# Seven block products for eight in the last 1x1 convolution of four images

## The chip, the cores and the metric

The kernel runs on one core of a Trainium2 chip, in fp32. A core has TensorE (matrix products into PSUM, an accumulator memory of 8 banks of 128 x 512 fp32), VectorE, ScalarE and GpSimd (the row POOL), and SyncE (SP); each takes its instructions in order from its own queue. Data moves between the chip's memory (DRAM) and the on-chip SBUF by DMA transfers that SP, ScalarE or POOL issue. The metric is the time of one execution on the device in microseconds (us), median of several runs.

## What is computed

Two bottleneck layers follow one another on 16 images of 1024 channels and 32 x 32 pixels. The first has a local self-attention in its middle, the second a 3x3 convolution:

```python
def layer0(x):                                  # self-attention bottleneck
    h = relu(bn(conv1x1(x, w_conv1)))           # 1024 -> 256
    h = self_att(h, wq, wk, wv, ...)            # 3x3 neighbourhoods, softmax over 9 taps
    return relu(bn(conv1x1(h, w_conv3)) + x)    # 256 -> 1024

def layer1(x):                                  # convolution bottleneck
    out = relu(bn(conv1x1(x, w1)))              # 1024 -> 256
    out = relu(bn(conv3x3(out, w2)))            # 256 -> 256
    out = bn(conv1x1(out, w3))                  # 256 -> 1024
    return relu(out + x)                        # x is layer0's output
```

The change is in the last convolution of `layer1` (w3), its addition of the residual x and its relu. Per image that is a 1024 x 256 matrix (the norm's scale is multiplied into it beforehand) times 256 x 1024 pixels.

## The kernel before

**Tiling.** Channels lie on the 128 partitions. A chunk is 128 channels of 1024 channels, so an image's input, output or residual is 8 chunks of 128 x 1024. A 256-channel tensor is a tile of 128 x 2 x 1024. A product is 128 x 128 weights times 128 x 512 pixels (half an image).

**Stages and order.** Nothing is ordered by a compiler's scheduler: the kernel issues every instruction in the order of a written list, `stages` (L974): `P` an image's first convolution and projections, `F` the fused end of layer 0 with the beginning of layer 1 (`fused`, L1065), `W` the 3x3 convolution of four images at once in Winograd's form (`winograd_conv`, L747), `U` the last convolution of one image (`last_sum`, L1106). The list's last line is

```python
"F12 F13 F14 U10:0123 F15 U10:4567 U11:01234 W12 U11:567 U12 U13 U14 U15",
```

so after `W12` (images 12 to 15) come chunks 5 to 7 of image 11 and then four whole `U` stages. VectorE's long work (the softmax, the attention sums, the Winograd transforms) is put between these stages by a small planner, the class `Side`, that keeps two clocks of estimated time (`side.passes`, with an estimated 3.43 us per chunk, `CHUNK`). By `U12` it has nothing left to place.

**A chunk of the last convolution** (class `Expand`, L371). `seed` (L379) lets ScalarE copy the residual chunk from SBUF into a PSUM tile of 128 x 1024 (two banks; the pool `psum` has four such tiles, all of PSUM); `products` (L386) adds four products to it; `result` (L401) lets ScalarE add the norm's shift, clip at zero and write a tile of SBUF (`rpool`, four tiles), in another order of the pixels, and POOL issues the store. `last_sum` calls `seed` two chunks ahead; `seeds` (L1119) names the first two of the next stage, so that a stage's end preloads for the next. The very last chunk is split: ScalarE takes half (L412) and VectorE half (L413), with a store from ScalarE's and one from SP's queue (L414, L415).

**Residuals.** Layer 0's output goes to DRAM and comes back. `loads` is one list in order of use, of the inputs, the Winograd forms (`V`) and the residuals (`r`). `more_loads` (L314) issues the next loads on POOL's queue as long as a room is free; the rooms are the five tiles of `xpool` (`CHUNKS`), counted by `live`. `seed` frees a room as soon as its residual is copied.

**Weights.** `more_weights` loads weight tiles through SP's queue; the two halves of the last convolution's weights (`u3`) are in SBUF from `U10:0123` on and are kept to the end.

**Between.** `finish_winograd` (L860) lets ScalarE apply norm and relu to an image's hidden tile after the 3x3 convolution, two instructions of 128 x 1024 in place (L863). `run` (L1129) calls it one part before a `U` stage ends, for the image of the next one.

Of the kernel before, what the change touches and what calls it, by code (L numbers as in the profile page):

```python
# [72 lines left out]
def sa_bottleneck_kernel(ctx: ExitStack, tc: tile.TileContext, x, w1t, wqkvt, w3t, u1t, u2t, u3t, params, out):  # L73
# [11 lines left out]
    zpool = ctx.enter_context(tc.tile_pool(name="zpool", bufs=3))  # L85
    psum = ctx.enter_context(tc.tile_pool(name="psum", bufs=4, space=bass.MemoryType.PSUM))
    dram = ctx.enter_context(tc.tile_pool(name="dram", bufs=1, space=bass.MemoryType.DRAM))


# [224 lines left out]
    def more_loads():  # L314

        while loads and live[0] < CHUNKS + RESULTS - 1:
            kind, b, c = loads[0]

            spare = kind == "x" and b < 2 and c >= CHUNKS
            if live[0] >= CHUNKS and not (kind == "x" and b < 2):  # L320
                return
# [11 lines left out]
            name = f"{kind}_{b}_{c}".translate(str.maketrans(" ,", "__", "()"))  # L333
            if spare:
                t = rpool.tile([P, HW], F32, tag="r", name=name)
            else:
                t = xpool.tile([P, NK * 2 * PART], F32, tag="x", name=name)
                t = t if kind == "V" else t[:, :HW]

            (nc.scalar if kind == "x" and b == 0 else nc.gpsimd).dma_start(t, src)  # L340
            loaded[loads.pop(0)] = t
            live[0] += 1

    def free():
# [774 lines left out]
    def seeds(at):  # L1119

        if at < len(stages):
            kind, b, of = stages[at]
            if kind in ("fused", "u3"):
                return [(expand("w3" if kind == "fused" else "u3", b), o) for o in of[:2]]
        return []

    hooks = {}

    def run(at):  # L1129
# [8 lines left out]
        if kind == "fused":  # L1138
            parts, count = fused(b, of, then), 2 * NC
        elif kind == "u3":  # L1140
            parts, count = last_sum(b, of, then), len(of)
        elif kind == "conv1":
            parts, count = first_conv(b), NC
        elif kind == "qk":
            parts, count = projections.setdefault(b, project(b)), 5
        elif kind == "v":
            parts, count = projections[b], 2
        else:
            side.finish_firsts()
            parts, count = winograd_conv(b), 18  # L1150
        alone = kind not in ("fused", "u3")
        for part in range(count):
            if alone and then and part >= count - 2 and kind != "wino":
                into, which = then[part - count + 2]

                if which not in into.ahead:
                    into.seed(which)
            if made and (kind, part) in (("conv1", 4), ("u3", count - 2)):
                finish_winograd(made.pop(0))
            cost = next(parts)  # L1160
# [75 lines left out]
```

## Time and profile before

| | |
|---|---|
| median of 3 runs | 2411.03 us (2407.73 to 2412.01) |
| profiled execution | 2409.75 us |
| its span | 2408.0 us |
| TensorE (PE) busy | 2380.5 us, 99% of the span |
| VectorE (DVE) busy | 2080.2 us, 86% |
| ScalarE (ACT) busy | 919.2 us, 38% |
| POOL busy | 466.0 us, 19% |
| `U12` to `U15` on TensorE | 2293.3 to 2403.2 us |
| a residual's load, from issue to landing | median 5.6 us |

The span is the time between the first and the last instruction of the profiled execution. In rows of instructions, `out<-in` are tiles, then comes the shape, then the count; at the end stands the idle time before it and what released it. PEld is the loading of weights into TensorE, which overlaps the products. An fp32 product is two passes, so it stands twice in the counts. In the slices each digit is the busy share of a fortieth of the span in tenths.

### The profile page before, as it was taken

The numbers are of one execution on the slowest core, as the hardware profiler recorded it, in microseconds if no ns is written. First come the engines' busy times: TensorE is split into PE (matmuls) and PEld (weight loads), VectorE is DVE, ScalarE is ACT, GpSimd is POOL, SyncE is SP. The second block draws the span as 40 slices with busy tenths as digits, with TensorE's granted clock in tenths as the row PEclk, the third lists the DMA queues.
The fourth block names the chain that finished last, engine by engine and source line by source line (L and its number), as shares of the span: only waits on it lengthen the run. The fifth ranks groups of instructions, "written<-read, shape, count | busy, mean of one in ns | idle before, by whom it ended". The sixth has DMA issues, their size and how long they took to land.

```text
span 2408.0 us, 18460 instructions
## 1 busy us (share of the span) xinstructions
PE 2380.5 (99%) x6144; PEld 1152.8 (48%) x6144; DVE 2080.2 (86%) x1648; ACT 919.2 (38%) x889; POOL 466.0 (19%) x854
## 2 busy tenths in 40 slices
PE   8999999999999999999999999999999999999999
PEld 3444444444476444444476444444476444434844
DVE  4799999999999999998999999999989999873700
ACT  3323241333122574442122574334122553344265
POOL 2111111111111232111111231111111221112132
PEclk9999999999999999999999999999999999999999
DMA  9979686888798897777898997787798986788887
GB/s 352 356 225 312 244 284 216 264 296 261 276 327 272 321 398 292 234 262 238 244 316 295 300 406 276 249 285 263 241 324 297 322 329 228 243 286 271 320 298 252
DMA packets 296126, 691.04 MB, mean 287 GB/s; under 512 B 20064, under 2 KB 166496, under 8 KB 287584
## 3 DMA queue, kind: packets, MB, share of 16 engines
q0 software_dynamic: 119024, 471.40, 54.4%
q1 hardware_dynamic: 175568, 213.97, 28.2%
q10 hardware_dynamic: 1440, 4.51, 0.5%
q8 instruction: 49, 0.80, 0.1%
q14 instruction: 45, 0.37, 0.0%
HBM read 416.09 MB, written 273.70 MB: 286 GB/s over the span
## 4 chain that ended last, share of the span: by engine, by line
PE 85%; DVE 5%; DMA 4%; issue 4%; POOL 1%; ACT 1%; SPq 0%; POOLq 0%; ACTq 0%; DVEq 0%
PE ps L358 35%; PE ps L390 29%; PE ps L454 11%; PE ps L771 9%; DVE acc L631 2%; DVE acc L649 1%; PE ps L492 1%; DMA a<-a 1%; DMA U<-uw 1%; POOL out_dram L418 1%; DMA a<-acc 1%; POOL r L340 1%; DMA uw<-u 0%; DMA s<-in_x_dram 0%; DMA v<-v 0%
## 5 line engine op out<-in xcount | busy, mean ns | idle before, releaser
L390 PE MATMUL ps<-a,w 128*128 128x512 f32 x1024 | 461.6, 596 | 5.8 <-ACT a L675 5.8
L358 PE MATMUL ps<-result,u 128*128 128x512 f32 x1024 | 459.9, 595 | 4.0 <-ACT result L417 4.0
L358 PE MATMUL ps<-x,w 128*128 128x512 f32 x1024 | 444.5, 595 | 6.4 <-DMA x<-in_x_dram 6.4
L390 PE MATMUL ps<-y,u 128*128 128x512 f32 x1024 | 441.2, 593 | 1.0 <-ACT ps L381 1.0
L631 DVE TENSOR_TENSOR acc<-e,bnv 128x2048 f32<-128x2048 f32 x144 | 327.6, 2283 | 34.1 <-ACT e L613 31.0
L574 DVE TENSOR_TENSOR prod<-qc,bnk 128x2048 f32<-128x2048 f32 x144 | 324.1, 2288 | 1.7
L417 ACT ACTIVATE result<-ps,par 128x1024 f32<-128x1024 f32 x128 | 142.4, 1113 | 462.2 <-PE ps L390 393.6
L390 PEld LDWEIGHTS ps<-a,w 128*128 128x128 f32 x1024 | 195.7, 191 | 253.9 <-issue 243.2
L358 PEld LDWEIGHTS ps<-x,w 128*128 128x128 f32 x1024 | 195.7, 191 | 251.9 <-issue 251.6
L358 PEld LDWEIGHTS ps<-result,u 128*128 128x128 f32 x1024 | 195.1, 191 | 250.5 <-issue 237.5
L390 PEld LDWEIGHTS ps<-y,u 128*128 128x128 f32 x1024 | 194.8, 190 | 245.6 <-issue 240.8
L649 DVE TENSOR_TENSOR acc<-acc 128x2048 f32<-128x2048 f32 x128 | 293.4, 2292 | 4.4
L454 PE MATMUL ps<-h,wqk 128*128 128x512 f32 x512 | 222.3, 592 | 0.0
L417 ACT ACTIVATE result<-ps,bn_sh 128x1024 f32<-128x1024 f32 x127 | 141.0, 1111 | 140.1 <-PE ps L390 139.6
L418 POOL DMA_DIRECT2D r<-result x128 | 68.8, 537 | 636.0 <-ACT result L417 620.5
L579 DVE TENSOR_TENSOR prod<-prod 128x2048 f32<-128x2048 f32 (+1 forms) x80 | 166.2, 2078 | 2.5
L454 PEld LDWEIGHTS ps<-h,wqk 128*128 128x128 f32 x512 | 97.3, 190 | 122.4 <-issue 109.9
L1037 ACT ACTIVATE h<-ps,par 128x1024 f32<-128x1024 f32 x32 | 38.5, 1203 | 279.1 <-PE ps L358 279.0
L381 ACT ACTIVATE ps<-r 128x1024 f32<-128x1024 f32 x128 | 130.5, 1020 | 27.1 <-DMA r<-r 19.6
L466 ACT ACTIVATE kp<-ps,par 128x1024 f32<-128x1024 f32 x64 | 77.4, 1209 | 156.4 <-PE ps L454 114.7
L381 ACT ACTIVATE ps<-s 128x1024 f32<-128x1024 f32 x128 | 131.1, 1025 | 2.5
L340 POOL DMA_DIRECT2D x<-in_x_dram x120 | 63.7, 531 | 301.0 <-PE ps L358 227.1
(317 smaller groups left out, 2296.6 us busy)
## 6 DMA issues: line engine op xcount, KB each, us to landing
s<-in_x_dram POOLq DMA_DIRECT2D x128, 512.0 KB, 6.3
r<-result POOLq DMA_DIRECT2D x128, 512.0 KB, 4.0
r<-r POOLq DMA_DIRECT2D x128, 512.0 KB, 6.5
out_dram<-result POOLq DMA_DIRECT2D x127, 512.0 KB, 6.2
x<-in_x_dram POOLq DMA_DIRECT2D x120, 512.0 KB, 5.1
v<-v SPq DMA_DIRECT2D x96, 408.0 KB, 4.6
U<-uw SPq DMA_DIRECT2D x72, 512.0 KB, 4.3
bnk<-kp SPq DMA_DIRECT2D x32, 680.0 KB, 7.7
```

Source lines behind the costliest of these rows:

```text
L340: (nc.scalar if kind == "x" and b == 0 else nc.gpsimd).dma_start(t, src)
L358: nc.tensor.matmul(ps[n][:, halves(half)], wt[:, c % (NC // 2), n * P : (n + 1) * P], src[:, halves(half)], start=(c == first), stop=(c == ...
L381: nc.scalar.activation(ps, loaded.pop((self.kind, self.b, o)), AF.Identity)
L390: nc.tensor.matmul(self.ahead[o][:, halves(half)], pieces[key][:, n, o % (NC // 2) * P :][:, :P], self.src[:, n, halves(half)], start=Fals ...
L417: nc.scalar.activation(to_, ps, RELU, bias=self.shift(o), scale=1.0)
L418: nc.gpsimd.dma_start(to, t)
L454: nc.tensor.matmul(ps[:, halves(half)], pieces[key][:, m, at : at + P], h[:, m, halves(half)], start=(m == 0), stop=(m == NW - 1),)
L574: nc.vector.tensor_tensor(by_row(t[:, two]), by_row(qc), kc[:, :, i : i + JROWS, j : j + W], ALU.mult)
L579: nc.vector.tensor_add(u[:, :, 0:4], u[:, :, 0:4], u[:, :, 4:8])
L631: nc.vector.tensor_tensor(by_row(dst), rows(e[:, k, :]).unsqueeze(1).to_broadcast([P, HEAD_DIM, JROWS, W]), vc[:, :, i : i + JROWS, j : j ...
L649: nc.vector.tensor_add(acc, acc, t)
L771: nc.tensor.matmul(acc[i][:, at, :, n, :], pieces[key][:, m, at, n * P : (n + 1) * P], v[:, at, :, m * (TILES + TR) :][:, :, :TILES], star ...
```

## The change

For images 12 to 15 two chunks of the output (256 channels, one *pair*) are computed together. Seen as blocks, a pair's weights are 2 x 2 blocks of 128 x 128 and the hidden tile is 2 x 2 blocks of 128 x 512 (two channel halves, two pixel halves). Four output blocks take eight products; the changed kernel uses Winograd's form of Strassen's scheme: seven products of sums of blocks.

- `late_weights`: at the start of `W12` VectorE makes the four sums of weight blocks (`s`) for all pairs, eight instructions. It also hands out SBUF that the attention no longer uses: four areas for sums of hidden blocks, five further rooms for residuals (`late_rooms`).
- `change`: VectorE makes an image's four sums of hidden blocks (t1 to t4, t4 in place of a block), for image 12 ahead of `U12`, for the others during the image before.
- `Pair`: products 1, 6 and 5 add up in one bank, 7 and 4 in another, 2 and 3 have one each; two such sets of four banks take the place of the pool `psum`, which is closed before `U12`. VectorE adds banks 1, 6, 5 (twice), 7, 4 and 2 into the residual tiles in SBUF. Product 3 is added to a half residual that ScalarE copied into its bank, and ScalarE copies the sum back. `result` then reads the residual tile. Product 5 of a pair and its results come after product 1 of the next pair. The last pair of all has an order of its own, and its product 2 adds to a half copied into the bank.
- `late_sums` takes the place of `last_sum` and of the preloads (`seeds`) for these images, and calls `finish_winograd` for the next image at an image's first pair.
- `free_late`: a residual's room comes free when its result is issued.

```diff
--- before.py
+++ after.py
@@ -83,8 +83,9 @@
     apool = ctx.enter_context(tc.tile_pool(name="apool", bufs=1))
     ppool = ctx.enter_context(tc.tile_pool(name="ppool", bufs=2))
     zpool = ctx.enter_context(tc.tile_pool(name="zpool", bufs=3))
-    psum = ctx.enter_context(tc.tile_pool(name="psum", bufs=4, space=bass.MemoryType.PSUM))
     dram = ctx.enter_context(tc.tile_pool(name="dram", bufs=1, space=bass.MemoryType.DRAM))
+    sums_room = ExitStack()
+    psum = sums_room.enter_context(tc.tile_pool(name="psum", bufs=4, space=bass.MemoryType.PSUM))
     par = const.tile([P, _NPAR], F32, tag="par", name="par")
@@ -315,9 +316,10 @@
         while loads and live[0] < CHUNKS + RESULTS - 1:
             kind, b, c = loads[0]
+            late = kind == "r" and b >= B - NK
             spare = kind == "x" and b < 2 and c >= CHUNKS
-            if live[0] >= CHUNKS and not (kind == "x" and b < 2):
+            if live[0] >= CHUNKS and not (kind == "x" and b < 2) and not (late and late_rooms):
                 return
             if kind == "V":
@@ -331,7 +333,10 @@
             else:
                 src = x[b, c * P : (c + 1) * P, :]
             name = f"{kind}_{b}_{c}".translate(str.maketrans(" ,", "__", "()"))
-            if spare:
+            if late and live[0] >= CHUNKS:
+                t = late_of[loads[0]] = late_rooms.pop(0)
+                live[0] -= 1
+            elif spare:
                 t = rpool.tile([P, HW], F32, tag="r", name=name)
             else:
                 t = xpool.tile([P, NK * 2 * PART], F32, tag="x", name=name)
@@ -340,6 +345,16 @@
             (nc.scalar if kind == "x" and b == 0 else nc.gpsimd).dma_start(t, src)
             loaded[loads.pop(0)] = t
             live[0] += 1
+    late_rooms, late_of = [], {}
+    def free_late(key):
+        if key in late_of:
+            late_rooms.append(late_of.pop(key))
+        else:
+            live[0] -= 1
+        more_loads()
     def free():
@@ -1120,10 +1135,164 @@
         if at < len(stages):
             kind, b, of = stages[at]
-            if kind in ("fused", "u3"):
+            if kind == "fused" or (kind == "u3" and b < B - NK):
                 return [(expand("w3" if kind == "fused" else "u3", b), o) for o in of[:2]]
         return []
+    blocks, changes = {}, {}
+    def late_weights():
+        s = apool.tile([P, KK, JPIX], F32, tag="e", name="s").rearrange("p a b -> p (a b)")[:, : 4 * HALF]
+        s = s.rearrange("p (s q o) -> p s q o", s=4, o=P)
+        at = [(kind, b) for kind, b, of in stages].index(("u3", B - NK))
+        for half in range(2):
+            a = pieces["u3", owner[at, "u3", half], half].rearrange("p n (q m o) -> p n m q o", m=2, o=P)
+            s1, s2, s3, s4 = (s[:, i, 2 * half : 2 * half + 2] for i in range(4))
+            a11, a12, a21, a22 = a[:, 0, 0], a[:, 1, 0], a[:, 0, 1], a[:, 1, 1]
+            nc.vector.tensor_tensor(s1, a21, a22, ALU.add)
+            nc.vector.tensor_tensor(s2, s1, a11, ALU.subtract)
+            nc.vector.tensor_tensor(s3, a11, a21, ALU.subtract)
+            nc.vector.tensor_tensor(s4, a12, s2, ALU.subtract)
+        blocks["s"] = s
+        rooms = [
+            apool.tile([P] + shape, F32, tag=tag, name=tag).rearrange("p d w -> p (d w)")
+            for tag, shape in (("bnv", [HEAD_DIM, HALO]), ("bnk", [HEAD_DIM, HALO]), ("qc", [HEAD_DIM, JPIX]),
+                               ("pc", [NPOS, JPIX]))
+        ]
+        rooms.append(kp.rearrange("p n r w -> p (n r w)"))
+        hidden_ = vh.rearrange("p r w -> p (r w)")
+        for k, t in enumerate(rooms[:3] + rooms[4:]):
+            changes[B - NK + k] = t[:, : 3 * HALF].rearrange("p (t w) -> p t w", t=3)
+        late_rooms.extend([rooms[0][:, 3 * HALF :][:, :HW], rooms[1][:, 3 * HALF :][:, :HW], rooms[3]])
+        late_rooms.extend([hidden_[:, :HW], hidden_[:, HW : 2 * HW]])
+    def change(b):
+        y, t = hidden_one[b], changes[b]
+        b11, b12, b21, b22 = (y[:, n, halves(half)] for n in range(2) for half in range(2))
+        t1, t2, t3 = (t[:, i] for i in range(3))
+        t4 = b12
+        nc.vector.tensor_tensor(t3, b22, b12, ALU.subtract)
+        yield
+        nc.vector.tensor_tensor(t1, b12, b11, ALU.subtract)
+        yield
+        nc.vector.tensor_tensor(t2, b22, t1, ALU.subtract)
+        yield
+        nc.vector.tensor_tensor(t4, b21, t2, ALU.subtract)
+        blocks[b] = {1: b11, 2: b21, 3: b22, 4: t4, 5: t1, 6: t2, 7: t3}
+        yield
+    class Pair:
+        def __init__(self, b, q):
+            self.b, self.q = b, q
+            self.end = (b, q) == (B - 1, NC // 2 - 1)
+            tiles = [banks.tile([P, HALF], F32, tag=f"ps{i}", name="ps") for i in range(4)]
+            self.banks = dict(zip((1, 6, 5, 7, 4, 2, 3), (tiles[i] for i in (0, 0, 0, 1, 1, 2, 3))))
+            self.r = [loaded.pop(("r", b, 2 * q + m)) for m in range(2)]
+            nc.scalar.activation(self.banks[3], self.r[0][:, HALF:], AF.Identity)
+        def add(self, m, half, ps):
+            to = self.r[m][:, halves(half)]
+            nc.vector.tensor_tensor(to, ps, to, ALU.add)
+        def product(self, i):
+            ps = self.banks[i]
+            a = pieces[piece("u3", self.q // 2)]
+            o = self.q % 2 * 2 * P
+            if i in (1, 2, 4):
+                w = {1: a[:, 0, o : o + P], 2: a[:, 1, o : o + P], 4: a[:, 1, o + P : o + 2 * P]}[i]
+            else:
+                w = blocks["s"][:, {5: 0, 6: 1, 7: 2, 3: 3}[i], self.q]
+            by = blocks[self.b][i] if i > 3 else hidden_one[self.b][:, i > 1, halves(i == 3)]
+            nc.tensor.matmul(ps, w, by, start=i in (1, 2, 7) and not (i == 2 and self.end), stop=True, skip_group_check=True)
+            if i == 1 or (i == 2 and not self.end):
+                self.add(0, 0, ps)
+                if self.end:
+                    nc.scalar.activation(self.banks[2], self.r[0][:, :HALF], AF.Identity)
+            elif i == 6:
+                self.add(1, 0, ps)
+            elif i == 5:
+                self.add(1, 1, ps)
+                self.add(0, 1, ps)
+            elif i == 7:
+                self.add(1, 1, ps)
+            elif i == 4:
+                self.add(1, 0, ps)
+            elif i == 3:
+                nc.scalar.activation(self.r[0][:, HALF:], ps, AF.Identity)
+        def result(self, m):
+            o = 2 * self.q + m
+            t = rpool.tile([P, HW], F32, tag="r", name="result")
+            to = out[self.b, o * P : (o + 1) * P, :]
+            r_, t_ = self.r[m].rearrange("p (j n) -> p j n", j=4), t.rearrange("p (n j) -> p j n", j=4)
+            shift = bn_sh[:, 2 * NW + o : 2 * NW + o + 1]
+            if self.end:
+                one, two = slice(0, 2), slice(2, 4)
+                if m == 1:
+                    nc.scalar.activation(t_[:, one], r_[:, one], RELU, bias=shift, scale=1.0)
+                    self.product(5)
+                    self.product(2)
+                    nc.scalar.activation(t_[:, two], r_[:, two], RELU, bias=shift, scale=1.0)
+                    nc.sync.dma_start(to, t)
+                else:
+                    ps = self.banks[2].rearrange("p (j n) -> p j n", j=2)
+                    nc.vector.tensor_scalar(t_[:, two], r_[:, two], shift, 0.0, ALU.add, ALU.max)
+                    nc.scalar.activation(t_[:, one], ps, RELU, bias=shift, scale=1.0)
+                    nc.scalar.dma_start(to[: P // 2], t[: P // 2])
+                    nc.sync.dma_start(to[P // 2 :], t[P // 2 :])
+            else:
+                nc.scalar.activation(t_, r_, RELU, bias=shift, scale=1.0)
+                nc.gpsimd.dma_start(to, t)
+            free_late(("r", self.b, o))
+    banks = None
+    def late_sums():
+        nonlocal banks
+        sums_room.close()
+        banks = ctx.enter_context(tc.tile_pool(name="banks", bufs=2, space=bass.MemoryType.PSUM))
+        last_one, next_one = None, Pair(B - NK, 0)
+        next_one.product(1)
+        for b in range(B - NK, B):
+            steps = iter(())
+            for q in range(NC // 2):
+                this = next_one
+                if q == 0 and b < B - 1:
+                    finish_winograd(b + 1)
+                    steps = change(b + 1)
+                if last_one:
+                    last_one.product(5)
+                    for m in range(2):
+                        last_one.result(m)
+                for i in (7, 6, 3, 4) if this.end else (7, 2, 6, 3, 4) if last_one else (2, 3, 7, 6, 4):
+                    this.product(i)
+                if this.end:
+                    this.result(1)
+                    this.result(0)
+                else:
+                    for _ in range((0, 1, 2, 1)[q]):
+                        next(steps, None)
+                    next_one = Pair(*((b, q + 1) if q + 1 < NC // 2 else (b + 1, 0)))
+                    next_one.product(1)
+                last_one = this
+                yield 6.0
+    late = late_sums()
     hooks = {}
     def run(at):
@@ -1137,6 +1306,8 @@
         fetch_attended()
         if kind == "fused":
             parts, count = fused(b, of, then), 2 * NC
+        elif kind == "u3" and b >= B - NK:
+            parts, count = late, NC // 2
         elif kind == "u3":
             parts, count = last_sum(b, of, then), len(of)
         elif kind == "conv1":
@@ -1147,6 +1318,8 @@
             parts, count = projections[b], 2
         else:
             side.finish_firsts()
+            if b == B - NK:
+                late_weights()
             parts, count = winograd_conv(b), 18
         alone = kind not in ("fused", "u3")
         for part in range(count):
@@ -1155,8 +1328,12 @@
                 if which not in into.ahead:
                     into.seed(which)
-            if made and (kind, part) in (("conv1", 4), ("u3", count - 2)):
-                finish_winograd(made.pop(0))
+            if made and (kind, part) in (("conv1", 4), ("u3", count - 2)) and parts is not late:
+                one = made.pop(0)
+                finish_winograd(one)
+                if one == B - NK:
+                    for _ in change(one):
+                        pass
             cost = next(parts)
             if part == 0 and kind == "fused" and stages[at + 1][0] == "fused":
                 next_fused[0] = stages[at + 1][1]
```

## Prediction

> **What bounds the kernel now.** I read the busy shares and the slices first, then a table of busy time for each of the four images whose last convolution is touched, then the timeline at both ends of that stretch. The page:
>
> ```profile
> PE 2380.5 (99%) x6144; PEld 1152.8 (48%) x6144; DVE 2080.2 (86%) x1648; ACT 919.2 (38%) x889; POOL 466.0 (19%) x854
> ...
> PE   8999999999999999999999999999999999999999
> ...
> DVE  4799999999999999998999999999989999873700
> ...
> L390 PE MATMUL ps<-y,u 128*128 128x512 f32 x1024 | 441.2, 593 | 1.0 <-ACT ps L381 1.0
> ```
>
> TensorE sets the pace nearly everywhere, and VectorE, full for most of the run, shows 0 in the last two slices. Those are the last convolutions of images 12 to 15, the lines below (window, then busy us and count by engine, granted clock, DMA share, GB/s):
>
> ```profile
> core 0: us, PE busy (x) PEld busy (x) DVE busy (x) ACT busy (x) POOL busy (x), PEclk, DMA share, GB/s
> 2293.30:2320.80 27.50, 27.48 (x64) 12.28 (x65) 0.00 (x0) 20.18 (x20) 9.65 (x19) 1.00 0.89 309
> 2320.80:2348.20 27.40, 27.40 (x65) 12.18 (x64) 0.00 (x0) 18.43 (x18) 8.48 (x16) 1.00 0.90 307
> 2348.20:2375.70 27.50, 27.50 (x65) 12.18 (x64) 0.00 (x0) 18.43 (x18) 8.53 (x17) 1.00 0.90 307
> 2375.70:2403.20 27.50, 27.50 (x65) 11.98 (x63) 0.00 (x0) 14.42 (x14) 5.32 (x10) 1.00 0.57 214
> ```
>
> TensorE is busy all of it, at full clock, with no VectorE work at all. The 128 products (each is two passes, hence 64 records an image) run from 2293.32 to about 2403.18: 109.86 us, **0.858 us a product**, 3.43 a chunk of four. What waits at the front and at the back:
>
> ```profile
> 2289.26 2.50 DVE L838 TENSOR_TENSOR y<-z,y 128x512 f32<-128x512 f32 x4
> ...
> 2289.99 2.38 ACT L863 ACTIVATE y<-y,bn_sh,bn_inv 128x1024 f32<-128x1024 f32 x2 [2.26 <-DVE y L838]
> 2292.27 1.01 ACT L381 ACTIVATE ps<-r 128x1024 f32<-128x1024 f32 x1
> 2293.21 1.09 ACT L417 ACTIVATE result<-ps,bn_sh 128x1024 f32<-128x1024 f32 x1
> ...
> 2293.32 2.84 PE L390 MATMUL ps<-y,u 128*128 128x512 f32 x6 [1.05 <-ACT ps L381]
> ```
>
> ```profile
> 2403.55 0.69 ACT L412 ACTIVATE result<-ps,bn_sh 128x512 f32<-128x512 f32 x1 [2.32 <-PE ps L390]
> 2404.26 0.35 ACTq L414 DMA_DIRECT2D out_dram<-result  x1
> ...
> 2404.27 0.75 DVE L413 TENSOR_SCALAR result<-ps,bn_sh 128x512 f32<-128x512 f32 x1 [112.51 <-DMA out_dram<-result]
> ...
> 2405.04 0.34 SPq L415 DMA_DIRECT2D out_dram<-result  x1
> ```
>
> At the front ScalarE is behind, because the norm of image 12 waited for VectorE; TensorE idles about 1.1 us for the first preload. At the back 4.8 us lie between the last product and the span's end at 2408.0. ScalarE starts 0.32 to 0.37 after a product's end (2396.63 after 2396.32; 2403.55 after 2403.18): that is my handover from TensorE.
>
> **The change, part by part.**
>
> *Products.* Four images, four pairs each, 7 products for 8: 16 x 0.858 = **-13.73 us**, all on the path that sets the end. A pair takes 7 x 0.858 = 6.01 us.
>
> *VectorE's additions.* Seven per pair, 128x512, one operand in PSUM. Nearest row:
>
> ```profile
> L820 DVE TENSOR_TENSOR z<-z,ps x24: 678/680/689, 702.3 to 2287.9; 128x512 f32<-128x512 f32 x24
> ```
>
> 0.68 each, 4.76 a pair. The changed blocks of the next image (four subtractions, 0.69 by the row of y<-z,y) add one a pair on average: 5.45 of 6.01 us. In the third pair of images 12 to 14 there are two of them, 6.1 us, carried by the slack of its neighbours; back to back such rows start every 0.60, not 0.68, so even that one nearly fits. Cost nothing, covered by TensorE. It would set the pace from 0.75 us an addition.
>
> *Shared banks.* Products 1, 6, 5 add up in one bank and 7, 4 in another, and VectorE must read each partial sum before the next product. Here the Trainium skill speaks against the change: "PSUM — Partial Sum Buffer", section on bank collisions, says that two engines must be kept apart on a bank even where their elements differ. The tail agrees in kind: VectorE's half of the last chunk (2404.27) starts only as ScalarE's (ends 2404.24) is done. One handover is 0.32 + 0.68 + some 0.05 = 1.05 us. If nothing lay between, three a pair would cost 16 x 3 x 1.05 = 50 us, and the kernel would be 37 us slower. But two products lie between 7 and 4 (6, 3), and three or more between 1 and 6 and between 6 and 5: at least 1.72 us, so nothing is left. Only the very first pair has one product between 7 and 4: 1.05 - 0.86 = **+0.19**.
>
> *ScalarE.* Per pair two results (1.11 each), a half preload and a half copy back (some 0.65 each, by the 0.69 half at the tail), and a quarter of a norm (2.38): 4.1 of 6.0 us. In a norm's pair 5.9, but the norm is issued in the 2.5 us in which ScalarE waits for product 5 anyway. Nothing.
>
> *Front.* Images 12's preloads of whole chunks go; ScalarE does norm (to 2292.37), two results of image 11 (to 2294.5), then the half preload for product 3 (to 2295.15). Products 1 and 2 can run from 2292.1, product 3 not before 2295.2, so the stage behaves as if begun at 2295.2 - 1.72 = 2293.5, against 2293.32: **+0.16**. The banks are taken over from a closed pool: if the new one waited for the last result of image 11 as a whole, product 1 would start at 2294.55: +1.23. No row shows such a swap; dependences follow addresses elsewhere, so I take the low end. The change of image 12's blocks (4 x 0.60, from 2292.4) ends before product 6 asks.
>
> *Weight sums.* Eight additions of 128x256 at the start of the 3x3 stage (0.42 by the row of that size in the softmax): 3.4 us, inside a VectorE idle of 18.9 us there (2211 to 2230). Nothing; without the cover 3.4.
>
> *Residual rooms.* A residual is now held until its result is written, two pairs instead of one preload; ten rooms for five make up for it. The loads and stores are as many as before (33.6 MB), now over 96 us instead of 110: 349 GB/s if all fell inside. "DMA: Bandwidth & Descriptors", Specifications, gives about 358 GB/s of memory bandwidth per core: 93.7 us, only just under the products. The trace differs: 394 GB/s from 2300 to 2310, that is 85 us. And ten residuals instead of five come in ahead, from about 2275, when the other loads have all been issued; some 28 MB are left, 79 us by the page, 72 by the row. Nothing by either. On POOL's queue each free adds a load (0.53) behind a store that waits for the result: 2.1 of 6 us.
>
> *Tail.* Product 5 now ends one product ahead of the end E. VectorE adds it twice (E - 0.54 to E + 0.74), then its share of the last result 0.75: E + 1.5. ScalarE is done about then too. Last stores leave at E + 1.55 against 1.85 today, but 1 MB is in flight instead of 512 KB (the chunk before leaves at E + 0.85). With the 0.9 us from issue to first bytes and 400 GB/s, as seen at today's tail, bytes end at E + 4.4 and the span at about E + 5.45, against 4.8: **+0.65**, between -0.3 (the issue decides) and +1.4 (ScalarE and VectorE write interleaved elements of one tile and are put in order).
>
> *Sum.* -13.73 + 0.19 + 0.16 + 0.65 = **-12.7 us**. The profiled execution took 2409.75 (span 2408.0, 1.75 around it), so a like one would take 2397.0. The median of the runs shown is 1.28 above it; from 2411.03 I get **2398.3**.
>
> **Rivals.**
> (a) Handovers bind in each pair. If VectorE's queue puts the reads of 1 and 7 off by one product, each pair loses 2 x 0.19 = 0.4 us: 6 us, 2404.4. For it: VectorE is 90% full in these pairs and works in order. Against: 0.67 us of slack on the tightest handover.
> (b) Transfers become the bound. At today's 308 GB/s without the lead of the extra rooms, 33.6 MB take 109 us and the gain is gone: 2411. Half of it, 2405. For: DMA share is 0.90 already. Against: 5.6 us from a residual's issue to landing under today's load, and POOL idles for ScalarE: it is asked for no more.
> (c) Slower: weight loads come into the open. Today one wait stands before four products; now nearly each product has its own. If TensorE can't load the next weights while a wait stands ahead of it, one 0.19 load and a 0.05 wait event are exposed 112 times: 27 us, 2425. It decides from 12.7 / 112 = 0.11 us a product. Against: every fourth product waits today, and the weight loads go on each 0.43 across those waits; waits met early have cost nothing.
> (d) The products vanish but the front and the tail give back more: +1.2 and +0.8 on top, 2400.3. This is inside the forecast's own range.
>
> **How the numbers follow.** Forecast with (d) 0.77, own range 2396 to 2401; (a) 0.10; (b) 0.07; (c) 0.04; no more than the noise left for other causes 0.02. 0.2% is 4.8 us, about what a measurement of this kernel tells from no change. (a) and half of (b) still count as faster: 0.92; within 0.2%: 0.04; slower: 0.04. The runs before spread over 4.3 us, a median of three by perhaps 1.5 either way; so 2395.5 below, and up to (a) above: 2404.
>
> **What would show it.** Right: 224 matmul records for 256 in that stretch (some may be missing), spaced 0.43 without gaps; 112 additions from PSUM at 0.68 and VectorE near 80 to 90% there; a pair every 6.0 us; last product at about 2389.8; span near 2395. Wrong: TensorE idle before products 4 or 6 put down to VectorE (a); before a preload put down to a residual's transfer (b); weight loads spaced over 0.43 at each product (c).

## The result and the profile after

The changed kernel takes **2400.61 us** (median of 4 runs, 2397.26 to 2402.74) against 2410.28 (4 runs, 2407.73 to 2412.01) for the kernel before: a ratio of **0.9959**, 95% interval 0.9942 to 0.9977. A second measurement of the same two kernels gave 2400.67 against 2410.01, ratio 0.9966 (0.9954 to 0.9978). The forecast was 2398.3, range 2395.5 to 2404: sign and range hold, the gain is 8 to 10 us where 12.7 were expected. The profiled execution took 2399.24 us, its span 2397.5 (before: 2409.75 and 2408.0).

The page of the kernel after, busy shares and the slices of VectorE:

```profile
PE 2365.3 (99%) x6112; PEld 1143.9 (48%) x6112; DVE 2163.7 (90%) x1783; ACT 935.0 (39%) x891; POOL 465.8 (19%) x853
...
DVE  4799998999999999998999999999989999875687
```

32 matmul records fewer, 135 VectorE instructions more, and digits where the last two slices of VectorE's row showed 0. Busy time by window over images 12 to 15 (window, busy us and count by engine, granted clock, DMA share, GB/s):

```profile
core 0: us, PE busy (x) PEld busy (x) DVE busy (x) ACT busy (x) POOL busy (x), PEclk, DMA share, GB/s
2293.50:2317.50 24.00, 24.00 (x57) 10.38 (x56) 19.35 (x31) 16.46 (x14) 5.31 (x10) 1.00 0.59 202
2317.50:2341.50 24.00, 24.00 (x57) 10.48 (x56) 19.96 (x33) 22.09 (x19) 8.24 (x16) 1.00 0.96 338
2341.50:2365.50 24.00, 24.00 (x57) 10.49 (x56) 19.97 (x33) 22.15 (x19) 8.63 (x17) 1.00 0.98 348
2365.50:2390.00 24.50, 23.55 (x55) 10.07 (x53) 18.26 (x29) 21.78 (x20) 5.23 (x11) 1.00 0.64 251
```

An image now takes 24 us instead of 27.5, TensorE is still busy all of it, VectorE 83%. What was not forecast is ScalarE: 22.1 of 24 us, for an expected 4.1 of 6.0 a pair. The front and the back, in the timeline:

```profile
2287.87 2.37 ACT L878 ACTIVATE y<-y,bn_sh,bn_inv 128x1024 f32<-128x1024 f32 x2 [2.25 <-DVE y L853]
...
2290.15 2.09 ACT L432 ACTIVATE result<-ps,bn_sh 128x1024 f32<-128x1024 f32 x2
...
2292.30 1.12 PE L1219 MATMUL ps<-y,u 128*128 128x512 f32 x2 [2.13 <-ACT result L432]
```

```profile
2385.26 4.07 ACT L1258 ACTIVATE result<-r,bn_sh 128x1024 f32<-128x1024 f32 x2 [0.50 <-DVE r L1208]
...
2388.03 1.02 PE L1219 MATMUL ps<-y,u 128*128 128x512 f32 x2
...
2389.11 0.64 ACT L1234 ACTIVATE bnv<-ps 128x512 f32<-128x512 f32 x1
...
2391.59 1.14 ACT L1254 ACTIVATE result<-ps,bn_sh 128x512 f32<-128x512 f32 x1
...
2392.76 0.55 SPq L1256 DMA_DIRECT2D out_dram<-result  x1
2392.76 0.57 ACTq L1255 DMA_DIRECT2D out_dram<-result  x1
```

At the front TensorE idles 2.13 us, put down to the last result of image 11 (ScalarE does a norm, then two results, to 2292.24), twice the gap of before. At the back the last product starts at 2388.03; the last stores leave at 2392.76, because two results of the pair before (4.07 us for both) hold ScalarE to 2389.3.

**Where the time went.** I cut the end of each trace at four points: U, the end of image 11's last product (the first product's start less the idle time in brackets); F, the first product of image 12; E, the last product's start + 0.858 us; S, the end of the span.

| us | U to F | F to E | E to S | U to S |
|---|---|---|---|---|
| before | 1.05 | 109.86 | 4.82 | 115.7 |
| after | 2.13 | 96.59 | 8.61 | 107.3 |
| difference | +1.08 | -13.27 | +3.79 | -8.4 |
| forecast | +0.16 | -13.54 | +0.65 | -12.7 |

The other 2.1 us between the two spans lie ahead of U, where the kernels do the same but for the weight sums and some earlier loads: U falls anywhere from 2288.3 to 2297.5 in traces of kernels that are alike up to it. So the stretch from U, and not the span, is what I compare below.

### The profile page after: what moved, and what is told of

Same layout as the page of the kernel before. It is cut to its first block, busy times and chain, and to the rows that moved or that the text cites. A ratio compares the mean times of both kernels' runs of the same rounds, so it can differ in the third digit from the quotient of the medians.

```text
span 2397.5 us, 18521 instructions
## 1 busy us (share of the span) xinstructions
PE 2365.3 (99%) x6112; PEld 1143.9 (48%) x6112; DVE 2163.7 (90%) x1783; ACT 935.0 (39%) x891; POOL 465.8 (19%) x853
## 4 chain that ended last, share of the span: by engine, by line
PE 92%; DVE 3%; DMA 3%; ACT 1%; issue 1%; ACTq 0%; SPq 0%; DVEq 0%
PE ps L373 36%; PE ps L405 29%; PE ps L469 13%; PE ps L786 9%; PE ps L1219 4%; PE ps L507 1%; DVE acc L646 1%; DVE acc L664 1%; DMA a<-a 1%; DMA bnk<-kp 1%; DMA U<-uw 0%; DMA uw<-u 0%; DMA V__2_8221<-v 0%; DMA v<-v 0%; DVE form L715 0%
## 5 line engine op out<-in xcount | busy, mean ns | idle before, releaser
L405 PE MATMUL ps<-y,u 128*128 128x512 f32 x768 | 331.1, 592 | 0.0
L405 PEld LDWEIGHTS ps<-y,u 128*128 128x128 f32 x768 | 145.9, 190 | 183.3 <-issue 181.5
L432 ACT ACTIVATE result<-ps,bn_sh 128x1024 f32<-128x1024 f32 x96 | 106.6, 1112 | 102.5 <-PE ps L405 102.1
L809 ACT ACTIVATE z<-ps 128x1024 f32<-128x1024 f32 x48 | 49.2, 1025 | 178.1 <-PE ps L786 130.4
```

The costliest lines, as they stand in the source:

```text
L405: nc.tensor.matmul(self.ahead[o][:, halves(half)], pieces[key][:, n, o % (NC // 2) * P :][:, :P], self.src[:, n, halves(half)], start=Fals ...
L432: nc.scalar.activation(to_, ps, RELU, bias=self.shift(o), scale=1.0)
```

## The experiments

The theory after these views: the products save what they should; the new pool costs the front 1 us; at the tail it is ScalarE's results, 2.1 us each where I had taken 1.11. The rivals: the products themselves are only partly saved; the tail is a matter of bytes in flight or of POOL's queue; the extra rooms do nothing. All traces in one table (single runs have one time; "stores" is when the last stores are issued, after E):

| run | median us | U to F | F to E | stores | E to S | U to S |
|---|---|---|---|---|---|---|
| after | 2400.61 | 2.13 | 96.6 | 3.87 | 8.61 | 107.3 |
| after again | 2400.67 | 2.13 | 98.3 | 3.86 | 8.69 | 109.1 |
| e1_rows | 2399.07 | 2.12 | 96.9 | 3.03 | 8.2 | 107.2 |
| e4_eight | 2411.76 | 2.13 | 111.9 | 3.01 | 7.85 | 121.8 |
| e6_front | 2399.52 | 1.65 | 96.7 | 3.88 | 8.67 | 107.0 |
| e7_tail | 2403.03 | 2.13 | 98.6 | 2.07 | 8.41 | 109.2 |
| e8_plain | 2400.99 | 2.13 | 96.4 | 2.34 | 7.16 | 105.7 |
| e9_stores | 2403.33 | 2.13 | 96.6 | 3.88 | 8.87 | 107.6 |
| e10_ends | 2402.71 | 1.27 | 96.9 | 1.55 | 7.14 | 105.3 |
| e11_columns | 2400.15 | 1.26 | 96.9 | 1.54 | 7.18 | 105.3 |

The two with many waits inside: e2_old_pool 2421.68, U to S some 131; e5_five 2422.45, U to S 123.2.

**Eight products again.** Product 7 is issued twice; nothing else changes.

```diff
-            nc.tensor.matmul(ps, w, by, ...)
+            for again in range(2 if i == 7 else 1):
+                nc.tensor.matmul(ps, w, by, ...)
```

> The changed kernel with one product in each pair issued twice (product 7, which overwrites its bank both times), so eight products a pair and all of its other work. Theory 1 (TensorE alone sets the pace of the stretch, and everything else is hidden): 16 x 0.858 = 13.7 us more from the first to the last product, 96.6 to 110.3, and the kernel ends some 3 to 4 us later than the kernel before. Theory 2 (ScalarE at 22 of 24 us or VectorE at 20 of 24 is about to bind, and part of the saving is already eaten by it): less than 13.7 us more, because the added products fill waits.

The same product (3, in the timeline) of two pairs that follow each other, with the eighth product and then in the kernel after:

```profile
2344.74 1.02 PE L1220 MATMUL ps<-y,s 128*128 128x512 f32 x2
...
2351.60 1.02 PE L1220 MATMUL ps<-y,s 128*128 128x512 f32 x2
```

```profile
2344.17 1.02 PE L1219 MATMUL ps<-y,s 128*128 128x512 f32 x2
...
2350.18 1.10 PE L1219 MATMUL ps<-y,s 128*128 128x512 f32 x2
```

6.86 us against 6.01: a pair is eight or seven times 0.858, all else being the same. From F to E it took 15.3 us more, 13.7 for sixteen products and some 1.5 for a clock that fell at the start (below). TensorE alone sets the pace; within that clock's 1.5 us the gain of the stretch is its products, and without them the kernel is no faster than the one before (2411.76 against 2407.26 in that measurement).

**Where the front's microsecond comes from.** The banks become halves of two tiles of the old pool, which stays open:

```diff
-            tiles = [banks.tile([P, HALF], F32, tag=f"ps{i}", name="ps") for i in range(4)]
+            rooms = [psum.tile([P, HW], F32, tag="ps", name="ps") for i in range(2)]
+            tiles = [t[:, halves(half)] for t in rooms for half in range(2)]
```

> Only the banks of a pair change: they are halves of two tiles of the old pool of four PSUM tiles, which stays open, instead of tiles of a new pool opened once the old one is closed. Theory 1 (the swap of pools makes product 1 of the first pair wait for the last result of image 11): product 1 follows image 11's last product without a gap, product 3 waits about 0.9 to 1.1 us for its half preload instead, and TensorE's idle time there falls from 2.3 to about 1.1 us; from image 11's last product to the span's end 106.1 us for 107.3. Theory 2 (ScalarE's backlog alone sets the start, the swap only hides it): the third product starts as late as today, 4.5 us after image 11's last product begins to drain, and nothing is gained. A third outcome, products waiting for each other more often because two banks now share a tile, would show as gaps of over 0.1 us in every pair.

Product 1 now starts right behind image 11's last (2288.51, no gap); product 2 then waits 1.76 us for ScalarE's preload. So the gap is the pool's swap. But the waits of the weight loads in images 12 to 15 (who waited for whom, us in all, times, longest) changed too, in this run and then in the kernel after:

```profile
PEld ps L1219 <- DVE r L1208: 29.0, 39, 1.6
...
PEld ps L1219 <- DVE bnk L1208: 14.5, 12, 2.4
```

```profile
PEld ps L1219 <- DVE r L1208: 2.2, 8, 0.5
...
PEld ps L1219 <- DVE bnk L1208: 2.0, 5, 0.8
```

A product now waits for VectorE's read of the other half of its tile, as if a tile's two banks were one: pairs start 6.93 us apart (three of them 7.65) instead of 6.01, and the kernel is slower than before. The expectation had named this as its third outcome; the run says more on the handovers than on the front. U to S grew by 24 us, more than the change brings: some 16 from the second pair on, and some 9 up to there, where the granted clock stood at 0.50 (2296 to 2304) behind waits of 0.8 to 1.8 us. With the next edit as well (four runs):

> Both edits, the contiguous results and the banks in the old pool. If each of the two causes is real and they lie at different ends of the stretch, the gains add: 1.2 at the front and 2.4 to 2.8 at the back, from image 11's last product to the span's end 103.3 to 103.8 us instead of 107.3, and the median near 2397 when the changed kernel's is 2400.6. If the long tail has another cause than ScalarE's long results (more bytes in flight at the end), the back gives less than 1 us and the sum stays above 105.

2419.31 us (2415.87 to 2425.53), ratio to before 1.0044 (1.0027 to 1.0061). The second edit is lost in it.

The other way at the front leaves the pools alone: the norm of image 12 moves behind image 11's last but one result, and the last result is split between ScalarE and VectorE.

```diff
-            if made and (kind, part) in (("conv1", 4), ("u3", count - 2)) and parts is not late:
+            if made and (kind, part) in (("conv1", 4), ("u3", count - (1 if made[0] == B - NK else 2))) and parts is not late:
...
+                nc.scalar.activation(to_[:, :, one], ps[:, :, one], RELU, bias=self.shift(o), scale=1.0)
+                nc.vector.tensor_scalar(to_[:, :, two], ps[:, :, two], self.shift(o), 0.0, ALU.add, ALU.max)
```

> The changed kernel, with three things moved at the front: the norm of image 12 is issued one chunk later, behind the result of image 11's chunk 6; the last result of image 11 is split between ScalarE and VectorE by banks; the sums of image 12's blocks are issued after that. If the gap before product 1 of the first pair is the wait for image 11's last result (the new pool of banks waits for the old one as a whole), then that result ends 0.32 + 0.72 us after the last product of image 11 and TensorE's gap falls from 2.3 to about 1.1 us; from image 11's last product to the span's end 106.1 for 107.3 us. If the gap has another cause (image 12's norm or block sums), it stays at 2 us or grows.

The gap shrank to 1.65 us only: VectorE's half (from 2291.60) started only as ScalarE's (to 2291.57) was done, though each half reads a bank of its own, so the split serves nothing. The move without the split, as in e10_ends below, leaves 1.27. What remains is the last result itself, 1.1 us, and its handover.

**Why ScalarE's results take twice as long.** Before, a result read PSUM at a stride and wrote SBUF in sequence, 1.11 us. Now it reads the residual in SBUF in sequence and writes SBUF at a stride of four pixels. First theory: it is the strided write. The edit turns the loop, with the same output:

```diff
-            r_, t_ = self.r[m].rearrange("p (j n) -> p j n", j=4), t.rearrange("p (n j) -> p j n", j=4)
+            r_, t_ = self.r[m].rearrange("p (j n) -> p n j", j=4), t.rearrange("p (n j) -> p n j", j=4)
```

> Only the order in which the results of a pair are walked changes: pixel by pixel with the four quarters innermost, so that the write into the result tile is contiguous and the read from the residual strided, instead of the other way round. Theory 1 (the strided write makes ScalarE's results 2.1 us instead of the 1.11 of the kernel before): results fall to 1.1 to 1.25 us each, ScalarE's busy time in a 24 us window of images 13 and 14 from 22.1 to about 14 us, and the time from the last product's end to the span's end from 8.6 to about 6 us, because the copy of product 3 no longer waits behind two results of 2.1. Theory 2 (the source in SBUF instead of PSUM makes them slow): results stay at 2.0 us or more and the end of the span does not move. By either, the products stay 0.858 us apart; from image 11's last product to the span's end 107.3 us today, 104.5 to 105.2 by theory 1, 107 by theory 2.

The result of before, the instructions on the residual's tile after, and the result with the loop turned (duration min/median/max in ns):

```profile
L417 ACT ACTIVATE result<-ps,bn_sh x43: 1094/1113/1114, 2189.5 to 2400.1; 128x1024 f32<-128x1024 f32 x43
```

```profile
L1208 DVE TENSOR_TENSOR r<-ps,r x54: 675/686/693, 2307.0 to 2384.5; 128x512 f32<-128x512 f32 x54
L1258 ACT ACTIVATE result<-r,bn_sh x15: 2102/2166/2189, 2315.8 to 2387.2; 128x1024 f32<-128x1024 f32 x15
```

```profile
L1258 ACT ACTIVATE result<-r,bn_sh x15: 2078/2101/2126, 2315.8 to 2387.6; 128x1024 f32<-128x1024 f32 x15
```

The theory fell: 2.17 became 2.10. (VectorE's additions stand at the forecast's 0.68.) Then both sides in sequence, which leaves images 12 to 15 in another order of pixels, with as much work:

```diff
-                nc.scalar.activation(t_, r_, RELU, bias=shift, scale=1.0)
+                nc.scalar.activation(t, self.r[m], RELU, bias=shift, scale=1.0)
```

> The changed kernel with the results of all pairs but the last written in the residual's own order of pixels: the reordering of pixels in quarters is left out there, so these outputs stand in another order. Both sides of ScalarE's instruction are then contiguous in SBUF. If it is the strided side in SBUF, whichever it is, that makes a result 2.1 us where the kernel before, reading PSUM with a stride, took 1.11: results fall to 1.19 us, the price of the norm of an image, which is contiguous on both sides. If SBUF as the source makes the price, they stay at 2 us. From the first to the last product nothing should move (ScalarE is hidden there: 95.7 us); the end should fall by 2 us, since the copy of product 3 comes forward.

```profile
L1258 ACT ACTIVATE result<-r,bn_sh x15: 1132/1137/1148, 2318.3 to 2389.6; 128x1024 f32<-128x1024 f32 x15
```

1.14 us. So it is not SBUF as the source, nor the write alone: a stride in SBUF on either side doubles the instruction, while the stride in PSUM before did not. E to S fell by 1.45 us with it. That is ScalarE's share of the tail; it cost nothing in the middle, where F to E is 96.4 for 96.6.

**The tail: ScalarE, POOL's queue or bytes.** VectorE takes one of the two late results, which is issued after product 3 of the last pair; the loop is turned as above.

```diff
+                if (self.b, self.q, m) == (B - 1, NC // 2 - 2, 1):
+                    nc.vector.tensor_scalar(t_, r_, shift, 0.0, ALU.add, ALU.max)
+                else:
+                    nc.scalar.activation(t_, r_, RELU, bias=shift, scale=1.0)
```

> The changed kernel with two things changed at the back: the second result of the last pair but one is made by VectorE, and issued after product 3 of the last pair instead of ahead of its first product; and results are walked so that writes are contiguous (0.72 to 0.85 us for 1.14 to 1.2 in the halves of the last pair). Theory 1 (the long end of the span is ScalarE's queue: two results of 2.1 us stand ahead of the copy of product 3, and the last additions and results wait for that copy): the copy starts at about 1.5 us before the last product's end instead of 0.2 us after it, the last stores are issued about 2.0 us after the last product's end instead of 3.9, and the span ends 6.0 to 6.7 us after it instead of 8.6. Theory 2 (the bytes in flight at the end set it): the stores go earlier but the span ends less than 1 us earlier.

The last stores left 1.8 us sooner after E, and the span's end gained 0.2. The timeline shows POOL issuing three stores in a bunch, after an idle time with no releaser:

```profile
2390.20 2.55 POOL L1262 DMA_DIRECT2D out_dram<-result  x3 [4.02 <-issue]
```

Such an idle time stands once near the end of each trace in which POOL issues these stores, the kernel before included (5.48 us there); in e2_old_pool and e4_eight the profile names a copy of ScalarE as its releaser. To take it away alone, the stores of image 15 go to SP's queue:

```diff
-                nc.gpsimd.dma_start(to, t)
+                (nc.sync if self.b == B - 1 and self.q > 0 else nc.gpsimd).dma_start(to, t)
```

> The changed kernel, with the stores of image 15's results (its first pair excepted) issued on SP's queue instead of POOL's. In the changed kernel's trace one of the last three stores on POOL stands some 2.5 us after its result is done while POOL waits for nothing that the profile shows (3.95 us of idle time before it), and the transfers are empty for about 1.5 us there, 10 us ahead of the end. Theory 1 (stores held back on POOL's queue crowd the last transfers): each store leaves within 0.1 us of its result, and the span ends 7.2 to 8.1 us after the last product's end instead of 8.6. Theory 2 (only ScalarE's late results count): the store leaves earlier and the end stays at 8.4 to 8.8 us, since the last two stores are issued as late as before, 3.9 us after the last product's end.

The stores leave as their results are done, and nothing is won (8.87): ScalarE is late anyway. Then the early norm, VectorE's share, the turned loop and SP's queue in one kernel:

> The changed kernel with both ends mended: the norm of image 12 issued behind the result of image 11's chunk 6 and its block sums after it (without the split of the last result); the second result of the last pair but one on VectorE after product 3 of the last pair, contiguous writes of results, and image 15's stores on SP's queue. If the three causes found are the right ones: TensorE's gap ahead of product 1 is 1.2 to 1.4 us instead of 2.3; the last stores leave 2.1 us after the last product's end instead of 3.9, with no other bytes waiting before them, and the span ends 5.2 to 6.0 us after it instead of 8.6; from image 11's last product to the span's end 103.0 to 104.2 us instead of 107.3, and the median some 3 to 4 us (0.13 to 0.17%) under that of the changed kernel in the same call. If the end is set by the bytes alone, it stays above 7 us after the last product's end.

The gap is 1.27 as expected and the last stores leave at E + 1.55, the very time of the forecast, but E to S is 7.14 where I expected 5.2 to 6.0. The transfers say why (GB/s in 40 slices of the last 7.1 us of that run, from 1.5 us before the last stores):

```profile
GB/s 369 438 438 370 415 369 392 438 392 415 369 392 462 392 392 369 392 346 300 208 277 277 162 231 92 208 277 438 392 208 0 0 0 0 0 0 0 0 0 0
```

They are full from the left edge on. Four results, 2.1 MB, come ready within some 3 us (2392.5 to 2395.5), since product 5 of the pair before, and so both its results, comes behind the last pair's product 1; the kernel before had 512 KB every 3.43 us. Nothing moves just ahead of them, until 2393.3, 0.7 us before E. An estimate from these numbers: 2.1 MB at 400 GB/s are 5.3 us, and 1.8 us without bytes follow to the span's end, which makes E + 6.4. The rest, 0.7 us, is that the last stores move slowly, 90 to 280 GB/s for some 1.4 us. They are cut by partitions, 64 each, where the kernel before cut by columns. So, with that cut changed back:

```diff
-                    nc.scalar.dma_start(to[: P // 2], t[: P // 2])
-                    nc.sync.dma_start(to[P // 2 :], t[P // 2 :])
+                    nc.scalar.dma_start(to[:, :HALF], t[:, :HALF])
+                    nc.sync.dma_start(to[:, HALF:], t[:, HALF:])
```

> The kernel of e10_ends with the last two stores cut by columns (128 partitions x 512 each, as the kernel before cuts its last chunk) instead of by partitions (64 x 1024 each). In e10_ends the span ends 5.59 us after these stores are issued and 7.14 after the last product; there the transfers run at about 400 GB/s until the two halves are alone and then at 90 to 280 GB/s for some 2.2 us, and the halves land 3.8 and 4.4 us after their issue. In the kernel before, with column halves, they land after 2.0 and 2.1 us at about 340 GB/s. Theory 1, the cut by partitions makes them slow: the last 512 KB take 1.5 instead of 2.2 us, last product to span end 6.4 us (6.2 to 6.6), and no stretch of a microsecond below 300 GB/s at the end. Theory 2, they are slow because they are the last bytes behind a full queue, whatever their cut: 7.0 to 7.3 us, and again some 2 us at around 220 GB/s. The median moves by under 1 us against e10_ends in either case, which separate medians can't tell: the trace decides.

The same view (last 7.0 us):

```profile
GB/s 398 398 398 421 421 398 398 374 374 374 468 445 398 374 351 374 445 340 375 398 374 374 351 363 375 152 23 23 23 35 0 0 0 0 0 0 0 0 0 0
```

Half of each theory. The slow stretch is gone, so the cut made it; but the end didn't move (7.18). What is left is 0.7 us at 23 GB/s, a sixteenth of the full rate. There the queue of ScalarE's store moves eight packets of 2 KB one behind the other, a sixteenth of that store's 128, and nothing else moves, as if one of the 16 engines had fallen behind; the stores land after 3.8 and 4.4 us in both runs. Why it falls behind, no run shows. The medians of e10_ends (2402.71, ratio 0.9965, 0.9952 to 0.9977) and e11_columns (2400.15, ratio 0.9955, 0.9940 to 0.9971) can't be told from the changed kernel's: 2 us from U to S are less than its runs differ among themselves (up to 7 us). Neither is shown to beat it in time.

**Five rooms.** The two lines that hand out the extra rooms are left out.

```diff
-        late_rooms.extend([rooms[0][:, 3 * HALF :][:, :HW], rooms[1][:, 3 * HALF :][:, :HW], rooms[3]])
-        late_rooms.extend([hidden_[:, :HW], hidden_[:, HW : 2 * HW]])
```

> The changed kernel without the five further rooms for residuals: the ten lines of the pair read from and are loaded into the five old rooms only. Theory 1 (the rooms are needed because a residual is now held for two pairs: a load can start only when a result of the pair before is issued, some 4 us into a pair, lands 6 to 7 us later, and is asked for some 8 us after the pair's begin): two or three us of TensorE's idle time in each pair from the second or third on, put down to additions that wait for a residual's transfer, 25 to 45 us in all, the kernel at 2425 to 2445. Theory 2 (the rival of the forecast in which transfers bind, rooms or no rooms): with the rooms the stretch is already at its transfers' pace, so without them little is lost, under 5 us. If residuals were prefetched far enough by five rooms, nothing is lost.

```profile
DVE r L1206 <- DMA r<-r: 25.3, 13, 3.3
...
PE ps L1217 <- DVE r L1206: 11.8, 13, 1.9
```

15.9 us more from U to S: VectorE waits for a residual, TensorE for VectorE, once in nearly each pair. The direction is as expected, the size half of the low end (TensorE idles 11.8 us for an expected 25 to 45), because one room waited for costs a pair 0.3 to 1.95 us and not a whole load. In the kernel after VectorE waits for a residual once, for 0.2 us. The rooms decide whether the change wins or loses.

## Why the prediction was right, and by how much not

- **Products, right.** -13.73 + 0.19 was forecast from F to E; -13.27 was measured, and the eighth product put back brings the pair back to 6.86 us. TensorE has one wait of its own in the whole stretch (the 2.13 us).
- **VectorE and shared banks, right.** Additions at 0.68, VectorE 5.0 us a pair for an expected 5.45, weight loads waiting for its reads 0.8 us at most, that one in the first pair, which I had priced. e2_old_pool shows a price of the kind that I had set against it, some 16 us of waits against my bound of 50.
- **Rooms and transfers, right, but closer than "nothing" sounds.** The middle ran at 338 to 348 GB/s and a DMA share of 0.96 to 0.98, and no product waited for it. Rival (b) is what e5_five did, and at 2422 it is worse than my 2411.
- **ScalarE, wrong in size, right in effect for the middle.** I carried the 1.11 us of a result from PSUM over to one that reads SBUF and writes at a stride. It is 2.17; the pair takes ScalarE 5.5 us instead of 4.1, which still fits into 6.01.
- **Front, the wrong end (+1.08 measured).** I named both: +0.16 if dependences follow addresses, and product 1 at 2294.55 if the new pool waits for image 11's last result as a whole. It does. From before's U at 2292.27, the gap of 2.13 gives 2294.40. The low end rested on no row; e2_old_pool, which keeps the pool, has no gap ahead of product 1.
- **Tail, the term that was most off:** +0.65 forecast, +3.79 measured, beyond my upper end of +1.4. Of the 3.16 us too little, 2.32 are the last stores (E + 3.87, not E + 1.55), and 0.84 the time from there to the end (4.74, not 3.9). The first is ScalarE's late results. But mending them, as e10_ends does beside the front and POOL's queue, leaves E to S at 7.14, still 1.7 above the forecast: I had 1 MB in flight and counted only the last pair's own, and 2.1 MB were. By the estimate above that makes 1 us of the 1.7; the slow cut, or in e11_columns the late eight packets, makes the rest.
- **Rivals.** (a) and (c) did not occur: weight loads still follow each other by 0.43 us. (d), front and tail give back more, is what happened, with the front some 0.9 on top of the forecast for its 1.2 and the tail some 3 for its 0.8. That its 2400.3 meets the median so closely is partly luck: the stretch alone gained 8.4 us, two thirds of the 12.7, and the rest of the first trace's gain lies ahead of U, where the change adds only the weight sums and some earlier loads.

## What to carry to other kernels

A duration belongs to a source, a destination and a stride, not only to an operation and a size: when an edit moves an operand from PSUM to SBUF, look for a row with the same sides before taking the old one. When work is taken off the bounding engine, write down the end anew: which results become ready in the last microseconds, on which engine, and how many bytes are still to go; a chunk that is finished one step later brings its bytes with it. Price a change of pool at the whole last user of the old one, unless a row shows otherwise.

## What the runs showed of the hardware

- **A stride in SBUF doubles ScalarE's time on 128x1024:** 2.10 to 2.17 us with either side strided, 1.14 with none, 1.11 with the strided side in PSUM. In the last pair's halves (128x512) the strided write took 1.2 us and the turned loop 0.85, so there the sides differ. VectorE's half took 0.70 with a strided write and 0.50 with a strided read. The Trainium skill, "SBUF — State Buffer", section "Door 1: The DMA port swizzle", says that SBUF gives full bandwidth only where accesses follow each other in the same line of 16 bytes; at a step of four fp32 pixels each lands in another line, and for ScalarE this agrees. It puts PSUM's line at 8 bytes and speaks of slower matmuls there; ScalarE's strided read of PSUM shows no cost (1.11 us).
- **A gap of 2 us can lower the granted clock.** In three of the eight traces with a gap of 2.12 or 2.13 us, and in none of the four with 1.05 to 1.65 us and no further waits, the clock fell behind it, at a cost of 1.5 to 1.7 us. In e5_five it stayed up behind the 2.13 us and fell behind a later gap of 1.95. The second trace of the changed kernel by window (granted clock third from the right):

```profile
2288.00:2292.00 4.00, 1.87 (x4) 0.83 (x3) 2.68 (x4) 3.97 (x5) 1.07 (x2) 0.83 0.48 196
2292.00:2296.00 4.00, 4.00 (x8) 1.56 (x8) 1.38 (x2) 2.30 (x4) 0.00 (x0) 0.74 0.39 157
```

  Its first four records took 3.67 us instead of 1.98, and F to E is 98.3 for 96.6. "TensorE: Matmul & The Clock Gate", section "HAM oscillation — how this bites in real kernels", puts the limit at gaps over about 3.4 us, by which no trace here should have lost time at this gap; its section "What's actually happening" says that the window of activity runs freely. That the same gap does it in some executions only would fit a free-running window, but here 2 us were enough.
- **Open:** POOL's 3 to 5.5 us without a releaser near the end, and why eight packets come last at a sixteenth of the rate. No run shows the cause of either.
